# Layer 3's expert dispatch split by batch, the first half moved into the attention stream; two weight loads of layer 0 ordered behind a store

## The chip, the cores and the metric

The kernel runs on one core of one Trainium2 chip. A core has TensorE (PE, with its weight loads shown as PEld), VectorE (DVE), ScalarE (ACT), GpSimd (POOL) and SyncE (SP), each with its own in-order queue of instructions, and 16 DMA engines that all queues share. The metric is the device time of one launch in microseconds, lower is better.

## The reference

Four layers work on x, 2 batches of 512 tokens with 256 features (1024 tokens in all), in float32. Each layer adds a cross attention and then a mixture of experts, both on a layer norm of x:

```python
x = x + _L0_xattn_ref(_layernorm(x), ctx_1024, ...)
x = x + _L0_ffn_ref(_layernorm(x), ...)      # 8 experts, best one
x = x + _L1_xattn_ref(ctx_1024, _layernorm(x), ...)
x = x + _L1_ffn_ref(_layernorm(x), ...)      # best one, and a shared expert
x = x + _L2_xattn_ref(_layernorm(x), ctx_1024, ...)
x = x + _L2_ffn_ref(_layernorm(x), ...)      # two best of 8
x = x + _L3_xattn_ref(_layernorm(x), ctx_1024, ...)
x = x + _L3_ffn_ref(_layernorm(x), ...)      # two best of 8
```

The last one is what most of the change is about:

```python
h = rmsnorm(x @ W_in.T, in_norm_w)
logits = h @ Wr.T
_, idx = jax.lax.top_k(logits + expert_bias, TOP_K)     # TOP_K = 2
g_topk = jax.nn.softmax(jnp.take_along_axis(logits, idx, axis=-1), axis=-1)
...
for e in range(8):
    oe = rmsnorm(silu(h @ Wg[e].T) * (h @ Wu[e].T) @ Wd[e].T, enorm_w[e])
    out = out + gates[:, e:e + 1] * oe
s_hat = rmsnorm(out, out_norm_w) @ W_out.T
```

Layer 3's attention has 16 heads of 16 features over 1024 context rows, with rotary keys and queries.

## The kernel before

**Tokens and experts.** The 1024 tokens stand in X as 8 tiles of 128 rows, tiles 0 to 3 the first batch, 4 to 7 the second. An expert layer doesn't compute all experts for all tokens. It sorts: the *dispatch* gives each pick (token, expert) a slot, scatters the token's row to that slot of a DRAM tensor xd, and the experts then work on tiles of 128 slots. The first 8 tiles (`front`) belong to the 8 experts, one each; what an expert has beyond 128 rows goes to overflow tiles, whose weights are fetched by an indirect load on POOL with the expert's row in `wrow`. `ALWAYS` overflow tiles are worked on without a test (13 in layer 3), the rest only if `used` says so.

**The dispatch of layer 3 before.** It follows the attention and is done for all 8 tiles in one string: layer norm (`normed`), transposes (`to_T`), the product with W_in (`ph`), squares and root (`rms`, whose roots are `recip_sqrt`, line 62), the scaled rows `h`, transposes again, `router_logits` (`pl`), `two_best`, `two_gates`, and `slots_of`: a matmul with the triangle `below` and eight with `ones` (`pr`) count how many picks of each expert stand before a token, from which come overflow, fronts, slots, `wrow` and `used`. `moe` then issues 16 indirect DMAs on POOL (line 429), one for each pick and tile. Ahead of the second pick's eight, DVE writes another index into the last column of `h`, which must wait for the first pick's scatter of that tile to land. The first expert tile reads its slots back (`xs`, line 455) after all scatters.

**The attention of layers 2 and 3, `attend16`.** It works on 8 groups (batch, 4 heads), 16 slots each for layer 3. PE's order is written out by hand (`pe_in_order`): in each slot two score matmuls of the first pass (line 1394; DVE takes the maxima, line 1404), two of the second pass of an earlier group (line 1451; ACT takes the exponentials, line 1452), and a product with the values (line 1427). All PE results except the product rotate through seven PSUM banks of one tag (`bank`). Between slots stand *pieces*: short steps of generators in a queue (`Pieces`), such as the next group's queries (`prep`: pq, rot) and, after the first batch's last group, its four output projections (`add_out`: po). After the last first-pass slot (128) some 18 slots of second pass remain, then the last group's end and the second batch's projections.

**Layer 0's experts.** They use half tiles for two experts at a time (`pair_tile`, the first matmuls at line 489) in turn with overflow tiles (`slot_tile`). Before them, the filler `first_batch` computes keys and values of layer 1 for the first batch (`ahead1`): PE into a bank, ACT copies to `sk` or `sv` (two buffers), and ACT's queue issues the store to `kd` or `vd`. The weights `w` have four buffers. Two are loaded early; for the third and fourth, an overflow tile's (POOL) and one of the second pair's (SP), `behind_slots` makes them wait for the first read of slots, so that this one is not behind them:

```python
tc.add_manual_dep(
    x, first_slots[0].name, ...,
    reason="not among the transfers that the first tile waits for",
)
```

Where a scheduler may choose, it orders each engine's instructions when the kernel is built.

Of the kernel before, what the change touches and what calls it, by code (L numbers as in the profile page):

```python
# [33 lines left out]
def tile_kernel(ctx: ExitStack, tc: tile.TileContext, d: dict, out: bass.AP):  # L34
# [49 lines left out]

    def norm_to(dst, src, norm, ts=None, split=False):


        t0, mv, r = norm
        if split:
            nb = small.tile([P, mv.shape[1]], F32, tag=f"nb{mv.shape[1]}", name="nb")  # L90
            nc.vector.scalar_tensor_tensor(nb, mv[:, :, 0], -1.0, r, ALU.mult, ALU.mult)
        for t in range(mv.shape[1]) if ts is None else ts:
            if split and t % 2:
                nc.scalar.activation(
                    dst[:, t0 + t, :], src[:, t0 + t, :], AF.Identity, bias=nb[:, t : t + 1], scale=r[:, t : t + 1]
                )
                continue
            nc.vector.tensor_scalar(
                dst[:, t0 + t, :], src[:, t0 + t, :], mv[:, t, 0:1], r[:, t : t + 1], ALU.subtract, ALU.mult
            )  # L100
# [102 lines left out]
    class Pieces:  # L203
# [14 lines left out]
        def share(self, places):  # L218

            self.due += max(self.left, 0) / places  # L220
            while self.due >= 1.0:
                self.due -= 1.0
                self()
# [6 lines left out]
    def run_stream(n_groups, slots, lag, unit, prep, steps):  # L230


        pieces = Pieces()
        t = 0
        while t < n_groups * slots + lag or pieces.queue:
            n, u = divmod(t, slots)
            if u == 0 and n + 1 < n_groups:
                pieces.add(prep(n + 1), steps(n + 1))
            unit(t, pieces)
            if u == slots - 1:  # L240
                pieces.drain()
            t += 1


    def bc8(a):
        return a[:, :, None].to_broadcast([P, TT, E])

    def rt(name, shape=(TT, E)):
        return small.tile([P, *shape], F32, tag=f"rt_{name}", name=name, bufs=1)

# [34 lines left out]
    def two_gates(lg, oh1, oh2):  # L285

        t = rt("pick")
        s = rt("sel", (2, TT))
        for i, oh in enumerate((oh1, oh2)):
            nc.vector.tensor_mul(t, oh, lg)  # L290
            nc.vector.tensor_reduce(s[:, i, :], t, AX.X, ALU.add)
        m = rt("selm", (TT,))
        nc.vector.tensor_tensor(m, s[:, 0, :], s[:, 1, :], ALU.max)
        for i in range(2):
            nc.vector.tensor_sub(s[:, i, :], s[:, i, :], m)
        nc.scalar.activation(s, s, AF.Exp)
        nc.vector.tensor_add(m, s[:, 0, :], s[:, 1, :])
        nc.vector.reciprocal(m, m)
        for i in range(2):
            nc.vector.tensor_mul(s[:, i, :], s[:, i, :], m)  # L300
        return [s[:, i, :] for i in range(2)]


# [104 lines left out]

    def moe(L, ps, hp, ep, rows, slots, wrow, used, F, act, glu, finish, filler=None, hold=None, between=None):

# [8 lines left out]

        put, out_of = [], []  # L420
        named = len(slots) == 2
        RW = D + named
        for i, si in enumerate(slots):
            if named and i == 0:
                nc.vector.tensor_copy(rows[:, :, D], c_tok)
            for t in range(TT):
# [7 lines left out]
                put.append(x)  # L434
        if filler is not None:
            filler()
        wd = d[f"{L}_experts"]
# [4 lines left out]
        def behind_slots(x):  # L442

            tc.add_manual_dep(
                x, first_slots[0].name, mybir.DependencyInfo(mybir.DependencyClass.Sync, mybir.DependencyReason.DATA),
                reason="not among the transfers that the first tile waits for",
            )

# [205 lines left out]
    def ahead1(ps, st, w, cT, b, part=slice(None)):  # L654

        if b == 0:
            kds["L1"] = dram.tile([B * 4 * P, S], F32, tag="L1kd", name="kd")
            vds["L1"] = dram.tile([B * S, 512], F32, tag="L1vd", name="vd")

        def values(pv, kt):  # L660
            r = slice(b * S + kt * P, b * S + (kt + 1) * P)
            mm2(pv, cT, r, w, slice(512, 1024))
            v = st.tile([P, 512], F32, tag="sk", name="sv", bufs=2)
            nc.scalar.copy(v, pv)
            nc.scalar.dma_start(vds["L1"][r, :], v)

# [4 lines left out]
        jobs += [("v", kt) for kt in range(8)]  # L671
        ahead(ps, st, "L1", w, cT, jobs[part], values)

    def ahead16(ps, st, L, params, nkt):
# [58 lines left out]
    def fill_slots():  # L733
# [15 lines left out]
        for to in todo:  # L749
# [7 lines left out]
            )  # L757
            ins = yield

    def psum(tags, name):  # L760
# [271 lines left out]
    with (  # L1032
# [3 lines left out]
        psum(2, "L0fps") as ps,  # L1036
    ):
        rw = load_rows(fp, d["L0_ffn_router_w"], "rw")
        rb = load_bc(fp, d["L0_ffn_router_b"], "rb")
# [15 lines left out]
        def first_batch():  # L1055
            to_T(ps, cT, C, CT, g_c, b_c, "g")
            ahead1(ps, hp, wkv, cT, 0)

# [238 lines left out]

    def attend16(L, params, nkt, causal, rotary, bias, first=None, late=None):

# [10 lines left out]
        with (  # L1310
# [196 lines left out]
            with pe_in_order():  # L1507
                while t <= NG * slots + LAG + 6 or pieces.queue:
# [26 lines left out]
                    if k == 6 and 0 < m < NG:  # L1535
                        divide(m - 1)
                        if groups[m - 1][1] == 3:
                            pieces.add(add_out(groups[m - 1][0]), 4)

                    if h == 0 and 0 < n <= NG:  # L1540
# [11 lines left out]
    with (  # L1552
# [3 lines left out]
        psum(2, "L1fps") as ps,  # L1556
    ):
        rw = load_rows(fp, d["L1_ffn_router_wT"], "rw")
        xn = normed(fp, False)
# [27 lines left out]
    pre, params = params16("L3", True, False)  # L1587
    ap = pre.enter_context(tc.tile_pool(name="L3a", bufs=1, reuse_waits="tile"))
    first = {}
    with (  # L1590
# [3 lines left out]
        psum(2, "L2fps") as ps,  # L1594
    ):
        rw = load_rows(fp, d["L2_ffn_gate_wT"], "rw")
        xT = fp.tile([P, 2, NT], F32, tag="xT", name="xT")
# [11 lines left out]
        yd = moe("L2", ps, hp, ep, xn, slots, wrow, used, 1024, AF.Relu, False, plain, next_keys, hold)  # L1609
        add_results(results(ap, yd, 0, 4), gates, X, range(4))  # L1610
        late = results(ap, yd, 4, 4), gates


    attend16("L3", params, 8, False, True, False, first, late)
    pre.close()
    ctxr.close()
    with (
# [4 lines left out]
    ):  # L1622
        w_in = load_rows(fp, d["L3_ffn_W_inT"], "w_in")
        w_out = load_rows(fp, d["L3_ffn_W_outT"], "w_out")
        rw = load_rows(fp, d["L3_ffn_WrT"], "rw")
        eb = load_bc(fp, d["L3_ffn_expert_bias"], "eb")
        inw = load_bc(fp, d["L3_ffn_in_norm_w"], "inw")
        onw = load_bc(fp, d["L3_ffn_out_norm_w"], "onw")

        def mean_squares(ss, src):  # L1630

            sq = hp.tile([P, D], F32, tag="sq", name="sq")
            nc.scalar.activation(sq, src, AF.Square, accum_out=ss)  # L1633

        def rms(t, w, t0, n):

            ss = small.tile([P, n], F32, tag=f"ss{n}", name="ss")
            for i in range(n):
                mean_squares(ss[:, i : i + 1], t[:, t0 + i, 0:D])
            r = recip_sqrt(ss, n, 1.0 / D, RMS_EPS)  # L1640
            for i in range(n):
                nc.vector.scalar_tensor_tensor(
                    t[:, t0 + i, 0:D], t[:, t0 + i, 0:D], r[:, i : i + 1], w, ALU.mult, ALU.mult
                )

        xT = fp.tile([P, 2, NT], F32, tag="xT", name="xT")
        to_T(ps, xT, normed(fp, False), TT)
        h = fp.tile([P, TT, D + 1], F32, tag="h", name="h")
        for t in range(TT):
            ph = ps.tile([P, D], F32, tag="mm", name="ph")  # L1650
            mm2(ph, xT, slice(t * P, (t + 1) * P), w_in, slice(0, D))
            nc.scalar.copy(h[:, t, 0:D], ph)
        rms(h, inw, 0, TT)
        hnT = fp.tile([P, 2, NT], F32, tag="hnT", name="hnT")
        to_T(ps, hnT, h, TT)
        lg = router_logits(ps, hnT, rw)
        lb = rt("lb")
        nc.vector.tensor_add(lb, lg, eb[:, None, :].to_broadcast([P, TT, E]))
        oh1, oh2 = two_best(lb)
        gates = two_gates(lg, oh1, oh2)  # L1660
        slots, wrow, used = slots_of(ps, [oh1, oh2], 15)

        def normalise(yo, y, w):
            ss = small.tile([P, 1], F32, tag="ss1", name="ss1")
            mean_squares(ss, y)
            r = recip_sqrt(ss, 1, 1.0 / D, RMS_EPS)
            nc.vector.scalar_tensor_tensor(yo, y, r[:, 0:1], w[:, 6144:6400], ALU.mult, ALU.mult)

        yd = moe("L3", ps, hp, ep, h, slots, wrow, used, 1024, AF.Silu, True, normalise)
        acc = fp.tile([P, TT, D], F32, tag="acc", name="acc")  # L1670
        outv = out.flatten_outer_dims().rearrange("(t p) f -> p t f", p=P)
        for t0 in range(0, TT, 2):
            add_results(results(hp, yd, t0, 2), gates, acc, range(2), True)
            rms(acc, onw, t0, 2)
            pt = ps.tile([P, 2, 2, P], F32, tag="mm", name="pt")
# [8 lines left out]
            nc.vector.tensor_add(X[:, t0 : t0 + 2, :], X[:, t0 : t0 + 2, :], po)  # L1684
            nc.sync.dma_start(outv[:, t0 : t0 + 2, :], X[:, t0 : t0 + 2, :])


# [170 lines left out]
```

## Time and profile before

| | us |
|---|---|
| median of 3 runs | 2259.86 (2259.75 to 2261.13) |
| the profiled execution | 2264.73 |
| its span, first to last instruction | 2262.7 |
| PE busy | 2070.5 (92%) |
| DVE busy | 1083.6 (48%) |
| ACT busy | 859.6 (38%) |
| POOL busy | 439.3 (19%) |
| layer 0's experts, first pair's first matmul | at 529.0 |
| layer 3's stream, eight groups | about 1634 to 1922 |
| layer 3's experts, first matmul | at 1994.7 |

The busy times are averages over stages with different limits, so they don't say which engine ends a stage. For that one looks at the stretch in question: the chain that ended last names at each moment what the end waited for, and the timeline shows each instruction with the idle time before it and what ended it. The mean granted clock of TensorE over the span is 0.95 of full speed; in stretches where it has little to do, it is about 0.5.

### The profile page before, as it was taken

To read this page: it belongs to the slowest core of one execution; us is meant where nothing else is said; L and a number is where in the kernel's file an instruction comes from. 1 tells how busy PE (TensorE), PEld (TensorE's weight loads), DVE (VectorE), ACT (ScalarE), POOL (GpSimd) and SP (SyncE) were. 2 spreads that over 40 slices of the span, in tenths; PEclk is the share of its full clock that TensorE was granted. 3 is DMA by queue.
4 is the path that set the end of the run, shared out by engine and by line. 5 is a ranking of instruction groups with operands and counts; after the bars stand their busy time and mean duration, and the time that the engine had idled before them with its cause. 6 is when DMAs were issued, how large, how long until landed. Compare 5 with 4: busy or idle time off the path is not lost. (4 is left out here: it accounts for less than half of the span.)

```text
span 2262.7 us, 29983 instructions
## 1 busy us (share of the span) xinstructions
PE 2070.5 (92%) x11532; PEld 1218.9 (54%) x11532; DVE 1083.6 (48%) x2157; ACT 859.6 (38%) x1645; POOL 439.3 (19%) x420
## 2 busy tenths in 40 slices
PE   7999999987998999999998998899699999579996
PEld 3444444353674444545586344599433333479995
DVE  7666666740125656655213884110377773322223
ACT  4444444421115565555112333222135556223333
POOL 2222223210012112111101122322123310111110
PEclk9999999988998999999899998999789999689998
DMA  4222222257945011001464512688310101547872
GB/s 129 71 62 75 71 75 58 87 208 298 372 146 121 29 34 39 21 11 65 142 231 146 202 35 79 221 310 312 104 47 30 34 15 25 248 180 297 321 303 64
DMA packets 111703, 300.72 MB, mean 133 GB/s; under 512 B 23232, under 2 KB 76224, under 8 KB 102848
## 3 DMA queue, kind: packets, MB, share of 16 engines
q1 hardware_dynamic: 76048, 159.30, 21.1%
q0 software_dynamic: 9888, 104.49, 11.9%
q10 hardware_dynamic: 25616, 34.90, 4.2%
q8 instruction: 97, 1.59, 0.3%
q14 instruction: 54, 0.44, 0.1%
HBM read 242.93 MB, written 47.66 MB: 128 GB/s over the span
## 5 line engine op out<-in xcount | busy, mean ns | idle before, releaser
L1452 ACT ACTIVATE p<-s 128x512 f32<-128x512 f32 (+3 forms) x384 | 185.9, 545 | 176.3 <-PE s L1451 114.8
L1394 PE MATMUL s<-kT,qT 32*128 32x512 f32 (+3 forms) x768 | 217.4, 612 | 8.7 <-DVE nm L1400 4.6
L132 PE MATMUL pa<-sT,w 128*128 128x128 f32 x1664 | 204.7, 278 | 8.0 <-DVE sT L466 3.7
L132 PEld LDWEIGHTS pa<-sT,w 128*128 128x128 f32 x1664 | 197.0, 193 | 16.4 <-ACT sq L1633 5.8
L561 PE MATMUL y<-w,hT 128*128 128x256 f32 x832 | 194.1, 386 | 7.2 <-ACT hT L551 3.3
L1451 PE MATMUL s<-qA,kT 32*128 32x512 f32 (+3 forms) x768 | 196.4, 587 | 1.2 <-ACT p L1452 0.9
L1404 DVE TENSOR_REDUCE mx<-s 128x1 f32<-128x512 f32 x256 | 163.6, 685 | 56.1 <-PE s L1394 35.5
L561 PEld LDWEIGHTS y<-w,hT 128*128 128x128 f32 x832 | 155.7, 193 | 30.0 <-DVE hT L558 5.2
L1139 ACT ACTIVATE p<-s,nm 128x512 f32<-128x512 f32 x192 | 129.5, 686 | 83.8 <-DVE nm L1136 83.8
L969 ACT ACTIVATE p<-s 128x1024 f32<-128x1024 f32 x128 | 124.1, 1021 | 89.9 <-PE s L964 89.9
L970 DVE TENSOR_SCALAR p<-p 128x1024 f32<-128x1024 f32 x128 | 107.3, 846 | 95.9 <-ACT p L969 95.7
L1136 DVE TENSOR_REDUCE nm<-s 128x2 f32<-128x1024 f32 x96 | 113.2, 1221 | 83.1 <-PE s L1132 83.1
L149 POOL TENSOR_TENSOR kT<-kT,turned 128x512 f32<-128x512 f32 x62 | 100.6, 1629 | 215.3 <-DVE turned L147 209.2
L975 DVE TENSOR_TENSOR acc<-acc,p 128x1024 f32<-128x1024 f32 x96 | 132.6, 1381 | 2.8
L895 PE MATMUL o<-p,v 128*64 128x512 f32 x512 | 125.9, 609 | 3.8 <-DVE p L970 3.8
L132 PE MATMUL pg<-sT,w 128*128 128x128 f32 x1056 | 129.0, 275 | 0.0
L964 PE MATMUL s<-qT,kT 64*128 64x512 f32 x512 | 127.2, 615 | 0.0
L558 DVE TENSOR_TENSOR hT<-act,pg 128x512 f32<-128x512 f32 x66 | 45.2, 688 | 167.9 <-PE pg L132 148.8
L132 PEld LDWEIGHTS pg<-sT,w 128*128 128x128 f32 x1056 | 123.6, 192 | 0.0
L148 POOL TENSOR_TENSOR kT<-kT,cos 128x512 f32<-128x512 f32 x62 | 87.9, 1427 | 134.7 <-DMA turned<-kT 61.2
L1427 PE MATMUL o<-p,v 128*32 128x256 f32 (+3 forms) x1280 | 106.6, 404 | 6.7 <-POOL p L1456 6.5
L1153 PEld LDWEIGHTS pt<-ident,p 128*128 128x128 f32 x768 | 85.9, 141 | 49.8 <-issue 24.7
(295 smaller groups left out, 3054.3 us busy)
## 6 DMA issues: line engine op xcount, KB each, us to landing
w<-in_L_experts_dram SPq DMA_DIRECT2D x8, 3200.0 KB
w<-in_L_experts_dram SPq DMA_DIRECT2D x8, 3072.0 KB
w<-in_L_experts_dram SPq DMA_DIRECT2D x8, 2048.0 KB
w<-in_L_experts_dram SPq DMA_DIRECT2D x8, 1536.0 KB
kd<-sk ACTq DMA_DIRECT2D x40, 256.0 KB
kT<-kd SPq DMA_DIRECT2D x16, 512.0 KB
turned<-kT SPq DMA_DIRECT2D x60, 128.0 KB
v<-vd SPq DMA_DIRECT2D x12, 512.0 KB
```

The source lines that it names most:

```text
L132: nc.tensor.matmul(ps_ap, lhsT[:, dc, lcols], rhs[:, dc, rcols], start=(dc == 0), stop=(dc == 1))
L561: nc.tensor.matmul(y, hT[:, f, :], w2[:, f, :], start=(f == 0), stop=(f == FT - 1))
L895: nc.tensor.matmul(G[n]["o"][64 * j : 64 * j + 64, :], V[g, b][:, kt, pr * P + 64 * j : pr * P + 64 * j + 64], p[:, j, :], start=(kt == 0) ...
L964: nc.tensor.matmul(s1[:, j, :], G[n]["kT"][r, kt * P : (kt + 1) * P], G[n]["qT"][r, :], start=True, stop=True)
L969: G[n]["exp"] = nc.scalar.activation(p, s1, AF.Exp, scale=0.125).ins
L975: nc.vector.tensor_add(G[n]["acc"], G[n]["acc"], p)
L1136: nc.vector.tensor_reduce(nm[:, qt, :, c], s1, AX.X, ALU.max, negate=True)
L1139: nc.scalar.activation(p[:, j, :], s1[:, j, :], AF.Exp, bias=nm[:, qt, j, c : c + 1], accum_out=l[:, qt, j, c : c + 1],)
L1394: nc.tensor.matmul(s1[:, :w], qT[r, qt * P : (qt + 1) * P], kT[r, c * 512 : c * 512 + w], start=True, stop=True)
L1404: nc.vector.tensor_reduce(mx[:, qt, j, c : c + 1], s1, AX.X, ALU.max)
L1451: nc.tensor.matmul(s2[:, qs], kT[r, kt * P : (kt + 1) * P], qA[r, qs], start=True, stop=True)
L1452: nc.scalar.activation(p[:, j, qs], s2[:, qs], AF.Exp, scale=0.25)
```

## The change

1. `behind_slots` adds a second dependency: the load also waits for the last of the stores that the filler issued (`stored[-1]`, the eighth value store of `ahead1`). In layer 0 this holds for the two loads named above.
2. Layer 3's dispatch becomes a class that works on one batch of four tiles. `dispatch3(0, ...)` is a generator that `attend16` puts into its pieces after the first batch's output projections, with one idle step (`gap`) after three of its stages. It is spread over the stream's last two groups of first-pass slots; its scatters are issued after them. `dispatch3(1, ...)` follows the attention, and works out how the second batch's rows fit behind the first's. `last` finds the overflow tiles' experts. Overflow tiles are handed out to the first batch first; their number stays the same.
3. What goes with it: W_in, the router's weights and two vectors are loaded before the stream, into a pool at the other end of the memory; the first batch's temporary tiles use the four buffers of the results loaded late (`yg`), which get a pool of their own; routing tiles come from the layer's pool and no longer from a permanent one.

In each engine's order, the first batch's steps now stand between attention slots on PE, about two slots apart. ACT loads its function table four times more, for two roots among the exponentials. On SP, layer 3's first key tiles go ahead of the rotated ones, and the fourth weight load of layer 3's experts stands behind the first three reads of slots. In layer 0 the slot read of the second pair stands ahead of its put-off load.

```diff
     def behind_slots(x):
-            tc.add_manual_dep(
-                x, first_slots[0].name, ...
-            )
+            for y in (first_slots[0], stored[-1]):
+                tc.add_manual_dep(
+                    x, y.name, ...
+                )
...
+    class Dispatch:
+        def wait(self, b):
+            for _ in range(self.gap if b == 0 else 0):
+                yield
+        def turned(self, dst, src, bank):
+            for dc in range(2):
+                pt = bank("pt")
+                for i in range(4):
+                    nc.tensor.transpose(pt[:, i * P : (i + 1) * P], src[:, i, dc * P : (dc + 1) * P], ident)
+                copy_alt(dc, dst[:, dc, :], pt)
+                yield
+        def norm(self, b, pool, bank, tags=("xn", "xT")):
+            S = self.S[b]
+            S["rows"] = pool.tile([P, 4, self.width], F32, tag=tags[0], name="xn")
+            norm_to(S["rows"][:, :, 0:D], X, norm_of(X, 4 * b, 4), d0=0)
+            yield
+            yield from self.wait(b)
+            S["xT"] = pool.tile([P, 2, 512], F32, tag=tags[1], name="xT")
+            yield from self.turned(S["xT"], S["rows"], bank)
+        def logits(self, b, srcT, w, bank):
+            pl = bank("pl")[:, 0 : 4 * E].rearrange("p (t e) -> p t e", e=E)
+            for t in range(4):
+                mm2(pl[:, t, :], srcT, slice(t * P, (t + 1) * P), w, slice(0, E))
+            self.S[b]["lg"] = rt_of_batch(b, "lg")
+            nc.vector.tensor_copy(self.S[b]["lg"], pl)
+            yield
+            yield from self.wait(b)
+        def to_slots(self, b, picks, bank):
...
+            nc.tensor.matmul(pr, below, oh[:, 4:9, :], start=True, stop=False)
+            for k in range(1, 5):
+                nc.tensor.matmul(pr, ones, oh[:, 4 - k : 9 - k, :], start=False, stop=(k == 4))
...
+            for i, si in enumerate(S["slots"]):
+                if named and i == 0:
+                    nc.vector.tensor_copy(rows[:, :, D], c_tok[:, 4 * b : 4 * b + 4])
+                for t in range(4):
+                    if i == 1:
+                        c = 4 * b + t
+                        nc.vector.tensor_scalar(rows[:, t, D:], c_tok[:, c : c + 1], float(NT), None, ALU.add)
+                    x = nc.gpsimd.indirect_dma_start(
+                        out=xds[self.L][0], out_offset=bass.IndirectOffsetOnAxis(ap=si[:, t : t + 1], axis=0),
+                        in_=rows[:, t, :], in_offset=None,
+                    ).ins
...
-            nc.scalar.dma_start(vds["L1"][r, :], v)
+            stored.append(nc.scalar.dma_start(vds["L1"][r, :], v).ins)
...
                         if groups[m - 1][1] == 3:
                             pieces.add(add_out(groups[m - 1][0]), 4)
+                            if dispatch is not None:
+                                pieces.add(dispatch(bank), 15)
...
+    far, dp = apart("L3d")
+    disp = Dispatch("L3", 2, 1)
+    w_in, rw = load_rows(dp, d["L3_ffn_W_inT"], "w_in"), load_rows(dp, d["L3_ffn_WrT"], "rw")
...
+    def dispatch3(b, pool, bank, tags, hpool):
+        S = disp.S[b]
+        yield from disp.norm(b, pool, bank, tags[:2])
+        h = S["rows"] = hpool.tile([P, 4, D + 1], F32, tag="h", name="h")
+        for k in range(2):
+            ph = bank("ph").rearrange("p (t f) -> p t f", t=2)
+            for i in range(2):
+                c = (2 * k + i) * P
+                mm2(ph[:, i, :], S["xT"], slice(c, c + P), w_in, slice(0, D))
+            nc.scalar.copy(h[:, 2 * k : 2 * k + 2, 0:D], ph)
+            yield
+        rms(pool, tags[2], h, inw, 0, 4)
+        yield
+        yield from disp.wait(b)
+        hT = pool.tile([P, 2, 512], F32, tag=tags[3], name="hT")
+        yield from disp.turned(hT, h, bank)
+        yield from disp.logits(b, hT, rw, bank)
+        lb = rt_of_batch(b, "lb")
+        nc.vector.tensor_add(lb, S["lg"], eb[:, None, :].to_broadcast([P, 4, E]))
+        picks = two_best_of_batch(b, lb)
+        S["gates"] = two_gates_of_batch(b, S["lg"], picks)
+        yield
+        yield from disp.to_slots(b, picks, bank)
+
+    attend16(
+        "L3", params, 8, False, True, False, first, late, lambda bank: dispatch3(0, ay, bank, ["yg"] * 4, dp)
+    )
...
+        all_of(dispatch3(1, fp, banks(ps), ["xn", "xT", "sq", "hT"], fp))
+        disp.last()
...
+        yd = moe(
+            "L3", ps, hp, ep, None, [], disp.wrow, disp.used, 1024, AF.Silu, True, normalise, sent=disp.put
+        )
```

## The prediction

> **What bounds the kernel now.** I read the page first: span 2262.7 us, TensorE (PE) busy 92% of it. Then the chain that ended last, for the order of the stages around the change, then the timeline of the two stages that it touches, and the busy time by stretches. All sums below are made against this one profiled execution. It took 2264.73 us (its span and 2.0 us around it), 4.9 us above the median of the runs, 2259.86; I take the difference that I work out off the median.
>
> First, layer 0's experts. The timeline, columns start, duration, engine, line and operation; in brackets the idle time before it and what ended it:
>
> ```profile
> 511.09 0.33 SPq L475 DMA_DIRECT2D w<-in_L_experts_dram  x1
> 511.09 0.36 ACTq L665 DMA_DIRECT2D vd<-sv  x1
> ...
> 511.98 0.98 POOL L536 DMA_INDIRECT w<-in_L_experts_dram,wrow  x1 [5.92 <-DMA vd<-sv]
> 512.36 0.33 ACTq L665 DMA_DIRECT2D vd<-sv  x1
> ...
> 528.40 0.59 ACT L664 COPY sv<-pk 128x512 f32<-128x512 f32 x1 [16.07 <-DMA vd<-sv]
> ...
> 529.03 3.68 PE L489 MATMUL pa<-w,sT 128*64 128x512 f32 x8 [12.13 <-ACT sv L664]
> ...
> 545.98 2.05 PE L132 MATMUL pa<-sT,w 128*128 128x128 f32 x16
> ```
>
> Two weight loads of 3.07 MB start at 511.1 and 512.0. The store of 256 KB issued at 511.09 lands only at 528.3, where the ones before it took 2.1 and 2.9 us. ACT's next copy needs its buffer, PE needs the bank that the copy frees, so PE stands still for 12.1 us.
>
> Second, layer 3. The chain that ended last (start, duration, step): the attention's groups begin at the pq rows; then the attention's end and the dispatch.
>
> ```profile
> 1730.10 1.91 PE pq L132 x4
> ...
> 1761.74 1.91 PE pq L132 x4
> ...
> 1793.39 1.91 PE pq L132 x4
> ...
> 1810.38 1.92 PE po L1487 x8
> 1815.79 1.92 PE po L1487 x8
> 1821.21 1.92 PE po L1487 x8
> 1826.62 1.92 PE po L1487 x8
> 1832.52 1.91 PE pq L132 x4
> ...
> 1950.86 7.01 PE pl L132 x32
> ...
> 1969.70 1.01 POOL xd L429
> ...
> 1988.77 2.51 DMA xd<-h,si
> 1991.40 1.98 DMA xs<-xd
> 1994.71 3.77 PE pa L132 x16
> ```
>
> A group takes 31.6 us, and 39.1 us where four projections of 1.92 us stand in it: 7.5 us more for 7.7 us of PE work. PE is the bound there. From the last sum of the attention (1930.72) to the first expert matmul (1994.69), 64 us, PE waits for a string of small steps.
>
> ```profile
> 1850.00:1860.00 10.00, 10.00 (x99) 3.03 (x91) 7.32 (x13) 5.94 (x12) 1.28 (x1) 1.00 0.01 2
> 1950.00:2000.00 50.00, 17.97 (x85) 16.70 (x84) 12.03 (x76) 4.45 (x6) 15.45 (x16) 0.51 0.41 161
> ```
>
> Columns: length, then busy us of PE, weight load, DVE, ACT, POOL, then granted clock, DMA share, GB/s. In the stream DVE has 27% and ACT 41% to spare; in the dispatch PE works 18 of 50 us at clock 0.51.
>
> **Part 1, layer 0: the loads wait for the last store.** The two loads (one on SP, one on POOL) move behind the eighth store. Undisturbed, copies and stores alternate at what the first four show: store 3 lands about 2.3 us after its issue, copy 5 at 513.4, copy 8 at 517.7 (its matmul ends at 516.6), store 8 issued 518.3, landed about 520.6. PE then starts the pair at about 517.4, 11.6 us earlier. The pair takes 13 us (the next two pairs: 13.6 and 12.8; this one took 17.0 at a lower clock and with waits), so PE wants the next tile at 530.5. That tile's weights are what was put off: both loads leave at 520.6, and the same two with the stores took 17 us before (511 to 528.5, 412 to 446 GB/s). They land at about 537. So the stall doesn't vanish: it is 6.5 us in front of the tile that began at 545.98, and the gain is 9 us. Behind the waiting load on SP stand the slot reads of later tiles (one read, that of the second pair, is moved ahead of it) and the second pair's other load. That one needs a buffer that is free at 530.5, shares the queues with its fellow, and lands near 551; the second pair, 561.06 before, finds it then. The 9 us stay. On POOL only later loads queue. Bounds: 0 (loads landing at 546) to 12.
>
> **Part 2, layer 3's tail: half the dispatch.** By steps, before -> after: last sum to first transpose 1.9 -> 2.3 (other rows stand between on DVE); transposes and copies 3.8 -> 3.2; W_in and squares, paced by ACT at 0.86 per tile, 8.6 -> 5.8; root and scaling 1.35 the same; transposes and copies 4.5 -> 3.1; logits 7.0 -> 3.5; two best 3.9 -> 3.7 (as many instructions, half as wide, 0.22 each); ranks, 18 -> 10 matmul records, 4.1 -> 2.4; slots 3.8 -> 5.4, since the second batch's string has 33 DVE rows to the first index in place of 22, at 0.16; scatters, 16 -> 8 at 1.27, from the first to the last issue 19.1 -> 8.9; last scatter to first expert matmul 5.9 the same. Sum 64.0 -> 45.6: gain 18.4 us. Bounds 16 to 20. One of four weight loads of layer 3 now stands behind three slot reads on SP. It is needed for tile 3, 33 us after the start, and such a load takes 11 us in the median, 21 at most: nothing, unless the reads themselves are late.
>
> **Part 3, layer 3's stream: the first batch is added.** PE: 16 transposes (nmT x4 takes 0.6) 2.4; W_in, 16 records as po, 3.8; logits, 16 records (32 take 4.17 in layer 2) 2.1; ranks, 10 records (18 take 2.1 there) 1.2. Sum 9.5 us at full clock, all on the bound. Eight scatters (10 us of POOL) and the index rows fall after the last first-pass slot. POOL has only one division behind them, needed at the stream's end some 18 us later; DVE, waiting for the scatters to land before it writes the second index, has a reciprocal behind it. If that cover fails, up to 7 us. DVE gets about 13 us of new work (the two blocks of small operations are 3.7 and 3.5), ACT 10.5, four table loads of 1.28 among them. Both fit the spare time of two groups on average (63 us: 17 and 26), but not locally: seven banks are turned over in under two slots (2 us each), and products need the exponentials of the slot before.
>
> [...] The trace, in layer 3's experts:
>
> ```profile
> 2008.06 1.28 ACT L62 ACT_TABLE_LOAD   x1
> ...
> 2009.35 0.20 ACT L62 ACTIVATE rsq<-rsq 128x1 f32<-128x1 f32 x1
> 2009.58 1.28 ACT L557 ACT_TABLE_LOAD   x1
> ...
> 2010.87 0.60 ACT L557 ACTIVATE act<-pa 128x512 f32<-128x512 f32 x1
> ```
>
> A root between exponentials holds ACT from 2008.06 to 2010.87, 2.8 us. [...] About 1 us of each blip is slack in a slot. [...] Stream: +13 us.
>
> [...]
>
> **Small edits.** The routing tiles change pools, which moves three memsets, and in layer 2 the scatter ahead of a POOL product; PE there has key projections until 1450, 11 us after the last scatter. Layer 3's stream loads key tiles ahead of the rotated ones, some 4 us later for those, needed about 30 us later. Four small loads of 0.4 MB go ahead of them. Cost 0, bounds -2 to +2.
>
> **Sum.** -9 - 18.4 + 13 = -14.4 us: 2245.5.
>
> **Rivals.**
> (a) The stall in layer 0 only changes its name: the put-off loads land at 546 or later, since three queues share the engines. For it: the loads were done 17 us before use, and now come just in time. Against it: two loads at 425 GB/s need 15 us and have 25. Gain 0 there: 2254.5.
> (b) Slower: the stream's seven banks. While DVE works through small operations or ACT reloads tables, no bank comes free, PE stands, and the time is not recovered because PE is the bound. If none of the new DVE and ACT work is hidden, the stream pays 9.5 + 13 + 10.5 = 33 us, the sum is +5.6: 2265.5. It decides once stalls pass 17.9 us. For it: in-order queues, and a DVE 73% busy. Against it: both fit on average, and PE's inserted steps stand two slots apart, so each input is done before its turn.
> (c) The stream absorbs more than the groups say (5 us in place of 13): -22.4, 2237.5.
> [...]
>
> **Chances.** Main 0.70 (own range 2239 to 2252), (a) 0.10, (b) 0.08, (c) 0.08, (d) 0.04. 0.2%, 4.5 us, is about what a measurement of this kernel can tell from no change. Faster: 0.70 + most of (a) + (c) = 0.87; same 0.05; slower 0.08. The range reaches to (c) and just past (a): 2237 to 2256.
>
> **What would show it.** Layer 0: idle before the first pa of the pair under 1 us, and about 6 us before the next tile's pa, ended by its weights. Stream: the two groups after the projections together 10 to 16 us longer than 63. Tail: 44 to 48 us from the last sum to the first expert matmul, with eight scatters. It is wrong if the expert tile of layer 0 starts no earlier than before, relative to the attention, or if those two groups take over 80 us.

## The result and the profile after

| | before | changed |
|---|---|---|
| median of 7 runs, us | 2259.75 (2257.26 to 2261.33) | 2272.15 (2267.51 to 2276.64) |
| the profiled execution, us | 2264.73 | 2273.33 |
| its span, us | 2262.7 | 2271.6 |

The ratio is 1.0055, 95% interval 1.0042 to 1.0068: 12.4 us slower, where 14.4 us faster was forecast. The same kernel was then run on four more chips, beside the kernel before each time, and there it was 6 to 10 us faster. So the question is what happened in the first comparison.

Layer 0 first, in the timeline of the changed kernel (start, duration, engine, line and operation; in brackets the idle time before it and what ended it):

```profile
510.96 0.33 ACTq L884 DMA_DIRECT2D vd<-sv  x1
...
512.48 1.94 PE L706 MATMUL pa<-w,sT 128*64 128x512 f32 x8 [0.56 <-issue]
...
513.67 0.33 ACTq L884 DMA_DIRECT2D vd<-sv  x1
...
515.71 0.33 SPq L692 DMA_DIRECT2D w<-in_L_experts_dram  x1
...
516.64 0.98 POOL L753 DMA_INDIRECT w<-in_L_experts_dram,wrow  x1 [15.55 <-DMA vd<-sv]
...
534.06 3.75 PE L133 MATMUL pa<-sT,w 128*128 128x128 f32 x16 [8.34 <-DMA w<-in_L_experts_dram,wrow]
```

The 12.1 us before the pair are gone (0.56), the last store leaves at 513.7, the loads follow it, and the stall is now 8.3 us before the tile. That is the mechanism foreseen.

Now layer 3, in the chain that ended last (start, duration, step), from the first batch's projections to the first expert matmul:

```profile
1815.59 1.93 PE po L1720 x8
1822.10 1.98 PE pq L133 x4
1847.49 1.92 PE ph L133 x8
1852.84 1.94 PE ph L133 x8
1875.99 1.90 PE pl L133 x16
1904.35 5.39 another core or an unknown queue
1911.93 2.01 PE s L1684 x4
...
1942.13 2.01 PE s L1684 x4
...
1950.05 8.25 PE po L1720 x32
...
1973.29 3.60 PE pl L133 x16
...
1996.17 2.48 DMA xd<-h,si
1998.77 2.13 DMA xs<-xd
2002.23 3.77 PE pa L133 x16
```

The dispatch's steps stand where they were expected, and the tail is short. What is new is a piece of 5.39 us that the profile can't name, and behind it score matmuls that follow each other every 3.0 us. In the timeline of that spot:

```profile
1903.25 1.10 ACT L1685 ACTIVATE p<-s 128x512 f32<-128x512 f32 x2
1903.75 1.13 PE L1684 MATMUL s<-qA,kT 32*128 32x512 f32 x4
...
1905.38 1.13 PE L1684 MATMUL s<-qA,kT 32*128 32x512 f32 x4
...
1907.00 0.96 POOL L480 DMA_INDIRECT xd<-h,si  x1 [0.31 <-issue]
...
1909.72 2.06 ACT L1685 ACTIVATE p<-s 128x512 f32<-128x512 f32 x4 [5.37 <-remote]
...
1910.37 1.56 PE L1660 MATMUL o<-p,v 128*32 128x256 f32 x8 [3.87 <-ACT p L1685]
1911.86 2.08 PE L1684 MATMUL s<-qA,kT 32*128 32x512 f32 x4
...
1914.88 2.08 PE L1684 MATMUL s<-qA,kT 32*128 32x512 f32 x4
```

ACT waits for PE's scores of 1903.75. They should be done by 1904.9. But the trace's record of PE's semaphore has a step at 1903.73 and the next one only at 1909.70, four within 0.2 us, and ACT starts 0.02 us behind that, at 1909.72. PE then waits for ACT. POOL, DVE and the DMA queues go on meanwhile. I call this *the hold*. Behind it each matmul takes twice as long: 2.08 us for four scores, 1.13 before.

The stretches (length, busy us of PE, weight load, DVE, ACT, POOL, granted clock, DMA share, GB/s), first of this execution, then of a later one of the same kernel on another chip (after_again below), which has no hold:

```profile
1900.00:1910.00 10.00, 6.48 (x48) 1.67 (x40) 0.87 (x5) 4.03 (x8) 6.13 (x7) 0.91 0.30 96
1910.00:1920.00 10.00, 9.63 (x40) 2.38 (x44) 0.00 (x0) 3.96 (x8) 1.27 (x1) 0.50 0.28 66
1920.00:1930.00 10.00, 10.00 (x46) 2.25 (x46) 0.00 (x0) 4.13 (x8) 0.00 (x0) 0.50 0.00 0
1930.00:1940.00 10.00, 10.00 (x42) 2.60 (x40) 0.00 (x0) 3.48 (x7) 0.00 (x0) 0.50 0.01 2
```

```profile
1900.00:1910.00 10.00, 9.98 (x74) 2.89 (x76) 0.87 (x5) 7.14 (x15) 5.78 (x6) 1.00 0.30 96
1910.00:1920.00 10.00, 10.00 (x74) 2.75 (x74) 0.00 (x0) 6.75 (x13) 1.26 (x1) 1.00 0.27 67
```

From 1920 to 1940 PE is busy 10 of 10 us, as it is without the hold from 1910 to 1920, but at half clock, with 42 to 46 records where the other has 74. In the stretch of the hold itself, 1900 to 1910, both moved 96 GB/s. From the query projection of the sixth group (pq) to the sum of the last group (sm), the stream takes 159.5 us before, 175.1 without the hold, and 197.3 here.

### The profile page after: what moved, and what is told of

Read it like the earlier page. It is cut to its first block, busy times and chain, and to the rows that moved or that the text cites. A ratio compares the mean times of both kernels' runs of the same rounds, so it can differ in the third digit from the quotient of the medians.

```text
span 2271.6 us, 30058 instructions
## 1 busy us (share of the span) xinstructions
PE 2084.6 (92%) x11534; PEld 1217.7 (54%) x11534; DVE 1095.2 (48%) x2226; ACT 862.3 (38%) x1644; POOL 439.2 (19%) x420
## 5 line engine op out<-in xcount | busy, mean ns | idle before, releaser
L1627 PE MATMUL s<-kT,qT 32*128 32x512 f32 (+3 forms) x768 | 223.4, 624 | 10.0 <-DVE nm L1633 4.5
L1684 PE MATMUL s<-qA,kT 32*128 32x512 f32 (+3 forms) x768 | 210.4, 623 | 1.5 <-DVE qA L1648 1.5
L1660 PE MATMUL o<-p,v 128*32 128x256 f32 (+3 forms) x1280 | 114.7, 431 | 10.5 <-POOL p L1689 6.6
L1627 PEld LDWEIGHTS s<-kT,qT 32*128 32x128 f32 x768 | 78.3, 193 | 68.1 <-issue 28.3
```

The source lines that it names most:

```text
L1627: nc.tensor.matmul(s1[:, :w], qT[r, qt * P : (qt + 1) * P], kT[r, c * 512 : c * 512 + w], start=True, stop=True)
L1660: nc.tensor.matmul(G[n]["o"][32 * j : 32 * j + 32, qs], G[n]["v"][:, kt, g % 2 * 4 + j, :], p[:, j, qs], start=(kt == 0 and half != 1), st ...
L1684: nc.tensor.matmul(s2[:, qs], kT[r, kt * P : (kt + 1) * P], qA[r, qs], start=True, stop=True)
```

## The experiments

Theory A: a hold of PE at the stream's end brings PE's clock down; the second pass alone doesn't bring it back; hold and half clock cost about 22 us. Without them the change does what was worked out. Rivals: the change itself is slower, through its steps on PE, DVE and ACT or through its scatters; or any hold costs as much, wherever it stands.

Times below are medians, and ratios are to the kernel before on the same chip, with 95% intervals.

**1. Each half alone: l0_only, l3_only, l0_only_2.** l0_only is the kernel before with the two dependencies of `behind_slots`; l3_only is the changed kernel with this edit:

```diff
-            for y in (first_slots[0], stored[-1]):
+            for y in (first_slots[0],):
```

> Before with layer 0's edit alone (two weight loads wait for the last store). Theory A, the traces of before and after: the first pair begins 16.6 us earlier and the tile after it 11.9 us earlier, and that stays to the end: 12 us faster than before, 2248. Rival: what stood at -12 behind layer 0 in the one trace was partly the clock of the stages around it: 0 to 6 us faster, 2254 to 2260.

> The changed kernel without layer 0's edit. Theory A (the stream of layer 3 lost 37 us in the traces, the tail gave back 19): 22 to 25 us slower than before, 2283, with PE at half clock for some 40 us at the end of layer 3's stream again. Rival (the half clock of that stretch was an accident of one execution): about 5 us slower than before, 2265, and 1.62 us for each slot of the second pass at the end.

> Before with layer 0's edit alone, once more, beside the changed kernel. Theory (layer 0 gives 7 us in the traces, layer 3 about 5): 4 to 7 us faster than before, and 0 to 5 us slower than the changed kernel where that has no hold. Rival (layer 3's part gives nothing): as fast as the changed kernel without the hold.

Layer 0 alone: 2253.35, ratio 0.9980 (0.9966 to 0.9994), and on another chip 2251.65, 0.9972 (0.9960 to 0.9984). Layer 3 alone: 2254.68, 0.9988 (0.9974 to 1.0002). So layer 0 gives 4.5 to 6.3 us in time. Layer 3's part is not 22 us slower, and its trace has neither hold nor half clock at the stream's end: its stream takes 175.1 us. That was the first sign that the program alone doesn't bring the hold.

**2. The changed kernel again: late_scatter, after_again, after_3, after_4.** late_scatter was to send the first batch's scatters only after the attention. But the order is chosen by the scheduler, which put them back: each engine has the same instructions in the same order as in the changed kernel. It is read here as another run of that kernel.

> The changed kernel with the first batch's eight scatters sent only after the attention, ahead of the second batch's dispatch; nothing is left out. Theory A (the scatters' traffic held PE from 1905.9 to 1910.4 and so brought the clock down for the last 37 us): the stream is 20 us shorter, the tail about 10 us longer, 2262. Rival B (the hold and the clock come from the dispatch's other steps, its blocks of small DVE operations and its roots): stream as in the changed kernel, tail 10 us longer, 2282.

> The changed kernel as it is, beside the other three on one chip. Theory A (in the first comparison of the two, 2272 against 2260, each execution of the changed kernel lost about 20 us to a hold of PE at the end of layer 3's stream and to the half clock behind it, and this goes with the chip or the hour, not with the program): where the profile shows no hold there, it is 6 to 12 us faster than before; where it shows one, 12 us slower. Rival (the program itself is slower): 12 us slower with or without a hold.

> The changed kernel once more, on whichever chip comes. Theory A (the hold at the end of layer 3's stream goes with the chip or the hour): either about 2250, 6 to 9 us faster than before, with slots of 1.62 us at the stream's end, or about 2272 with slots of 3.0 us behind a hold; nothing between. Rival (the first comparison was slow for another reason): a time or a profile that fits neither.

> The changed kernel on whichever chip comes. Theory A (the hold goes with the chip or the hour): about 2250 with slots of 1.62 us at the end of layer 3's stream, or about 2272 with a hold and slots of 3.0 us. Rival: a time between, or one of the two without its profile.

| run | time | ratio | sixth pq to sm |
|---|---|---|---|
| late_scatter | 2248.87 | 0.9957 (0.9944 to 0.9970) | 175.1 |
| after_again | 2251.55 | 0.9967 (0.9955 to 0.9979) | 175.2 |
| after_3 | 2250.16 | 0.9971 (0.9957 to 0.9986) | 175.0 |
| after_4 | 2249.75 | 0.9967 (0.9954 to 0.9980) | 175.1 |

Four chips, 57 executions from 2241.5 to 2258.0, no hold in any of the four traces. In the first comparison all 7 executions lay at 2267.5 and above. The rival "the program itself is slower" is out for chips that don't show the hold.

**3. A hold made on purpose: forced_hold, hold_mid.** One product of PE gets one more wait. In forced_hold it is the fourth slot of the last group's second pass, which waits for the eighth scatter:

```diff
+                        if dispatch is not None and (m, k) == (NG - 1, 3):
+                            tc.add_manual_dep(held[0], disp.put[7].name, ...)
```

> The changed kernel with one wait added: the attention product of the fourth slot of the last group waits for the eighth scatter of the first batch. This makes a hold of PE of about 5 us where the trace of the changed kernel had one. Theory A (such a hold brings the clock down, and the second pass alone does not bring it back): the slots behind it take 3.0 us in place of 1.62, and the time is 5 + about 17 = 20 us or more above the changed kernel's on the same chip. Rival (the clock comes back within 7 us, as elsewhere in the trace): 5 to 8 us above it.

2275.4, ratio 1.0074 (1.0052 to 1.0095), 23.9 us above after_again on the same chip. The timeline:

```profile
1905.53 1.13 PE L1686 MATMUL s<-qA,kT 32*128 32x512 f32 x4
1911.75 1.08 PE L1661 MATMUL o<-p,v 128*32 128x256 f32 x8 [5.10 <-DMA xd<-h,si]
1912.76 2.08 PE L1686 MATMUL s<-qA,kT 32*128 32x512 f32 x4
...
1915.78 2.08 PE L1686 MATMUL s<-qA,kT 32*128 32x512 f32 x4
```

5.1 us of waiting, then slots of 3.02 us to the end. The stream takes 197.4 us; the first comparison's took 197.3. In hold_mid the fifth slot of the fourth group's second pass waits for the third group's divisors, where both passes run:

```diff
+                        if dispatch is not None and (m, k) == (3, 4):
+                            for y in spreads[-4:]:
+                                tc.add_manual_dep(held[0], y.name, ...)
```

> The changed kernel with a hold of PE made on purpose in the middle of layer 3's stream, where both passes run: the product of the fifth slot of the fourth group's second pass waits for the four transfers that spread the third group's divisors, some 5 us. Theory A (both passes together bring the clock back, the second pass alone does not): the hold, and 3 to 7 us at half clock behind it: 6 to 10 us above the changed kernel's 2249 to 2252. Rival (any hold of that length costs the 24 us that the one at the end cost): 2273 to 2276.

```profile
1768.34 1.08 PE L1663 MATMUL o<-p,v 128*32 128x256 f32 x8 [8.22 <-DMA rec<-inv]
...
1771.37 1.08 PE L1663 MATMUL o<-p,v 128*32 128x256 f32 x8
...
1774.10 0.64 PE L1663 MATMUL o<-p,v 128*32 128x256 f32 x8
...
1775.90 0.64 PE L1663 MATMUL o<-p,v 128*32 128x256 f32 x8
```

This hold came out longer, 8.2 us, but the product takes 1.08 us only twice and 0.64 from the third slot on: the clock is back after some 6 us (0.68 from 1760 to 1770, 0.81 from 1770 to 1780, 1.00 behind that). 2260.92, ratio 1.0015 (1.0000 to 1.0031), some 11 us above the changed kernel's ratio elsewhere, a little more than expected and far from the rival's 24. Its stream takes 186.9 us, 11.8 above 175.1: the hold and 3.6 us. So the longer hold costs less than half of the shorter. It is the place that makes it dear: behind the hold where only the second pass runs, the half clock stayed (0.50 from 1910 to 1950 in forced_hold). That it is the mix of matmuls at the place, and nothing else there, is argued from these two places.

**4. Dense matmuls behind the hold: burst, burst_again, burst_4.** All three are the changed kernel with this:

```diff
+                    if dispatch is not None and m == NG - 1 and 2 <= k < 6:
+                        warm = bank("warm")
+                        for dc in range(2):
+                            nc.tensor.matmul(warm, ident, xT[:, dc, 0:512], start=(dc == 0), stop=(dc == 1))
```

> The changed kernel with eight added 128-row matmuls of 512 columns (two in each of four slots) in the last group's second pass; their result is not used. Theory A (the clock had fallen and stays down because the 32-row matmuls of the second pass alone do not bring it back; dense matmuls do): 3.5 to 7 us of added work, then slots of 1.62 in place of 3.02 us for the 12 that remain, 17 us back: about 10 us faster than the changed kernel, 2262. Rival B (the low clock has another cause and stays): 4 to 7 us slower than the changed kernel, 2277 to 2279.

> The changed kernel with eight dense matmuls in four slots of the last group, as before. Theory A: where the changed kernel beside it has the hold and the half clock, it is about 10 us faster than that; where it has none, 4 to 7 us slower, the price of the matmuls (in the run before it stood 6 us above the same program without them).

> The changed kernel with eight dense matmuls in four slots of the last group's second pass, beside the changed kernel. Theory A: about 10 us faster than that where it has the hold, 4 to 7 us slower where it has none.

2255.0, 2258.02 and 2257.29, ratios 0.9995, 1.0001 and 1.0001: 6.1, 6.5 and 7.5 us above the changed kernel beside each. None of these chips showed the hold, so whether dense matmuls would have ended the half clock was not tested. What they do show is the price of PE work in this stream: 4 x 2.0 us of added matmuls cost nearly all of their 8 us.

**5. Where the dispatch stands: end_scatter, l3_end, gap0.** end_scatter really puts the eight scatters behind the attention, by a dependency on its last sum:

```diff
+                    if b == 0:
+                        tc.add_manual_dep(x, ends[-1].name, ...)
```

> The changed kernel with the first batch's eight scatters and their rows of DVE behind the attention's last sum. Theory A (the scatters' traffic is what holds PE): no hold at the stream's end, in any execution, and a tail longer by what of the eight scatters (10 us) isn't hidden behind the second batch's norm, W_in and logits, 0 to 4 us. Rival (the hold does not come from the scatters): time as the changed kernel's plus 0 to 4 us, hold included where that has one.

2263.8, ratio 1.0022 (1.0010 to 1.0033), 12.3 us above after_again on that chip. Both expectations fell: I had hidden the scatters behind the second batch's work, but the index rows of DVE between them wait for landings, and stand ahead of that work on DVE. The tail grows from 43.4 to 58.8 us, and the stream keeps its 175.2: sent this late, the scatters take away what the dispatch in the stream gives. As this chip doesn't show the hold, the run says nothing of what the scatters have to do with it.

l3_end takes the first batch's dispatch out of the stream:

```diff
-        ... first, late, lambda bank: dispatch3(0, ay, bank, ["yg"] * 4, dp)
+        ... first, late
...
+        all_of(dispatch3(0, fp, banks(ps), ["xn0", "xT0", "sq0", "hT0"], dp))
         all_of(dispatch3(1, fp, banks(ps), ["xn", "xT", "sq", "hT"], fp))
```

> The changed kernel with the first batch's dispatch taken out of layer 3's stream and done per batch after the attention, ahead of the second's. Theory (the working of the prediction as the clean traces have it: the stream pays about 15 us for the first batch, the tail gets back about 20): the stream is 15 us shorter, the tail 20 us and more longer, so 5 to 12 us above the changed kernel. Rival (the in-stream part costs more than it gives): at or below the changed kernel's 2249 to 2252.

2258.5, ratio 0.9998 (0.9987 to 1.0009). The stream is back at 159.6 us, the tail is 67.4. Against the changed kernel's ratios on other chips it is 6 to 9 us slower, as the theory had it. gap0 sets the pause to nothing (`Dispatch("L3", 2, 0)`):

> The changed kernel with no pause between the dispatch's steps in the stream (a gap of 0 pieces in place of 1), so that its steps come about two slots earlier each. Theory: PE's 9.9 us of steps stay; less time stands between a step and the one that needs it, so PE waits up to 3 us more for DVE and ACT, and the scatters begin some 8 us earlier, partly where both passes still run: 0 to 3 us above the changed kernel on chips without the hold. Rival (the pause is only lost distance): same as the changed kernel.

2255.84, ratio 0.9992 (0.9985 to 1.0000), about 6 us above the changed kernel's ratio: more than expected. Its stretches:

```profile
1870.00:1880.00 10.00, 9.74 (x50) 2.54 (x42) 7.21 (x24) 3.37 (x8) 1.26 (x1) 0.70 0.08 27
1880.00:1890.00 10.00, 9.66 (x58) 3.85 (x58) 5.51 (x22) 3.06 (x6) 3.89 (x4) 0.61 0.12 41
```

The steps crowd, the clock is lower (0.70 and 0.61 over 20 us), and the stream takes 183.4 us in place of 175.1. The pause is worth its slots.

**6. The kernel before, again: before_again.**

> The kernel before, looked at a second time. Its first profiled execution took 2264.7, 5 to 7 us above its medians on three chips. Theory: that execution was a long one (228.6 us of its span at half clock, where the versions profiled since had 173 to 202), so some 4 us of what stands against it around layer 0 and again around layer 2's dispatch is not the change's: a second one should show the 12 us stall of layer 0 again and a total of 2257 to 2260. Rival: stretches and total as in the first, 2263 to 2266.

One execution of 2260.2, span 2258.3: 4.4 us shorter than the first trace. It is 7.5 us ahead at the first value store of layer 0 and has lost 3.4 of that by the end of layer 2. Layer 0's stall is there again (the pair's tile 38.6 us after the first value store, 38.2 in the first trace), and so are 159.5 us of stream and 64.1 of tail. Layer 3's stages repeat to 0.2 us, layer 0's from the first store on to 1.3 us; the total of the first trace was long ahead of them.

**7. Layer 0's stall before the tile: tile_first, tile_first_early.** In tile_first the second pair's load waits for the tile's weights too; in tile_first_early the tile's load doesn't wait for the store:

```diff
                 if s > 0:
-                    behind_slots(x)
+                    behind_slots(x, stored[-1], put_off[0])
...
-                    behind_slots(x)
+                    behind_slots(x, stored[-1])      # tile_first_early: behind_slots(x)
+                    put_off.append(x)
```

> The changed kernel with the second pair's weight load (on SP) waiting for the tile's weight load as well, so that the tile's 3.07 MB come alone behind the last store. In the traces of the changed kernel the two loads start at 515.7 and 516.6 and land together at 534, and PE stands for 8.3 us before the tile. Theory (the two loads share the engines, so one alone takes about half): the tile's weights land at 524 to 526, the stall before it goes, the second pair's loads land at 541 to 543 and are wanted at about 542: 6 to 8 us faster than the changed kernel, about 0.993 of before on a chip without the hold. Rival (the second pair's load, now late, becomes the stall): no faster than the changed kernel, 0.997.

> As the version beside it, but the tile's load no longer waits for the last store (it starts at 512, beside the stores), and only the second pair's load waits. Theory (a store is held up by each load beside it): one load beside the stores holds the pair up by about half of the 11.5 us that two did, some 6 us, while the tile and second pair come earlier: 0 to 5 us slower than the version beside it. Rival (one load beside the stores does them no harm): as fast or faster than the version beside it.

2272.82, ratio 1.0080 (1.0059 to 1.0100), and 2270.1, 1.0075 (1.0051 to 1.0098). The reason isn't layer 0. On this chip, the sixth of the experiments, the hold is back, in both traces. tile_first at its spot:

```profile
1914.79 2.06 ACT L1688 ACTIVATE p<-s 128x512 f32<-128x512 f32 x4 [5.37 <-remote]
...
1915.44 1.56 PE L1663 MATMUL o<-p,v 128*32 128x256 f32 x8 [3.85 <-ACT p L1688]
```

The same 5.37 us as in the first comparison; PE's semaphore stops 5.7 us after the first scatter's issue there and here; then slots of 3.0 us follow; both streams take 195.7 us, and all 12 executions lie between 2265.5 and 2278.3. Times can't judge the two versions of layer 0 then, only traces. With tile_first the tile starts 24.9 us after the first store in place of 30.8, but the second pair then waits for its own load, and the layer's last product comes 154.3 us after the first store in place of 149.5: the rival. With tile_first_early it is 149.2, no different from the changed kernel and ahead of tile_first: the rival again. The stall moves; that the two loads of 3.07 MB cost that much in any order is a reading, not shown.

## Why the prediction was wrong

By its own steps, in us against before. "Without the hold" is the five traces l3_only, late_scatter, after_again, after_3 and after_4 (layer 0 without l3_only); where they differ, their mean.

| step | forecast | without the hold | first comparison |
|---|---|---|---|
| layer 0, first store to last expert product | -9 | -7 | -6.3 |
| layer 3's start, last product of layer 2 to the sixth pq | 0 | +3.8 | +4.3 |
| stream, sixth pq to sm | +13 | +15.6 | +37.8 |
| tail, last sum to first expert matmul | -18.4 | -21 | -20.5 |
| layer 3's experts | 0 | +1 | +1.8 |
| sum | -14.4 | -8 | +17 |
| measured, by the ratio | | -6.5 to -9.7 (four chips) | +12.4 |

The last column is one profiled execution against another and the table leaves out the other stages, which together were 8 us shorter than in the long trace of before: the two spans differ by 8.9 us, the medians by 12.4.

**The step that failed** is the stream's, and in it the stalls. I costed each PE step "at full clock", added small stalls, and took it that a stall costs its own length. Here it didn't: the clock of the matmuls behind it fell too, from 1.00 before 1908.2 to 0.50 from 1910 to 1950. The +13 us have 3.5 us for stalls beside the 9.5 us of PE steps, and no run shows that figure: without the hold the stalls cost 5.7 us, and in the first comparison the stream's 37.8 us less 9.9 us of PE steps make 27.9 us of them, eight times as much. Behind a hold of 4 to 6 us, the slots left of the second pass went from 1.62 to 3.02 us: 1.4 us each, some 17 us, with the hold 22. forced_hold shows that size (197.4 us of stream) and hold_mid that it depends on the place. The hold itself was not among the waits that the prediction thought of, and its cause is open. Rival (b) came near in time for another reason: it had banks blocked by DVE and ACT, but without the hold all stalls together cost 5.7 us (15.6 less the 9.9 us of PE steps), far from the 17.9 at which it was to decide.

It could have been seen. Part 1 of the prediction counts a lower clock behind layer 0's stall (with waits, 17.0 us for a pair that otherwise takes 13); part 3 puts it at nothing. And in the trace of before, layer 3's stream begins with first pass alone, where PE runs its scores from 1642.3 to 1657.3 without a break:

```profile
1640.00:1650.00 10.00, 10.00 (x39) 5.26 (x40) 8.38 (x15) 0.59 (x1) 7.30 (x6) 0.84 0.00 0
1650.00:1660.00 10.00, 10.00 (x32) 5.11 (x28) 9.54 (x18) 0.59 (x1) 0.20 (x1) 0.50 0.65 211
```

The same of the changed kernel (after_again):

```profile
1640.00:1650.00 10.00, 10.00 (x32) 5.78 (x30) 10.00 (x18) 0.59 (x1) 0.00 (x0) 0.50 0.68 220
```

PE is busy 10.00 of 10.00 us in all three, and the clock goes down to 0.50 and stays there: in this attention a busy PE is no proof of a fast one, and the first pass alone didn't raise the clock there. (DVE, at 9.54 and 10.00, may set the pace there, so this stretch doesn't show what the half clock costs.) The prediction took the clock from the stretch in use (1.00 at 1850) and didn't ask what a stall at 1905, with the first pass over, would do to it.

**Point by point.**

- *Layer 0*: mechanism right, size a little off. PE starts the pair as forecast and takes 13 us for it; the loads take 18 us, not 16.5, and the stall before the tile is 8.3, not 6.5. Rival (a) fell.
- *Tail*: right, and a little better. 43.4 us where 45.6 was forecast (44 to 48), eight scatters in 8.9 us.
- *Roots*: the row was right. ACT is held 2.8 us by a root, as the row said, and PE waits 0.7 us beside the first and 1.2 beside the second, for DVE each time (after_again). The working has a slip: 2.8 us less the 1 us of slack, an estimate, is 1.8, so the two roots alone make 3.6 us, all of the 3.5 that the +13 us have for stalls, and nothing is left there for DVE's blocks.
- *Matmul busy time*: the groups were right (7.5 us more for 7.7 us of PE work before). 9.9 us of inserted steps cost 15.6, and the 8 us of burst cost 6 to 7.5. Rival (c) fell.
- *Small edits at 0*: missed. Layer 3's start costs 3.3 to 4.3 us in the traces of the table, 3.1 in l3_end's, and between 1.7 and 4.1 in the others with its new order. PE waits 1.0 us for maxima behind DVE's work on rotated keys, and half clock lasts 24 to 27 us there in place of 17 (after_again and before_again). How much of it each reordered load or row makes wasn't tried.
- *Range*: without the hold the medians, 2248.9 to 2251.6, lie inside 2237 to 2256; the time of the first comparison doesn't.

**What stays open.** What holds PE's semaphore was not found. It came in the one trace of the first comparison and in both on the sixth chip of the experiments, each time at the same spot of the scatters; it came in none on the five chips between, though five of those traces have the scatters in that spot and nothing added to the stream (l3_only, late_scatter, after_again, after_3 and after_4), and four of the five are of the very program that had it first. The kernel before, run beside those that had the hold, took its usual time each time (2259.75 in the first comparison, 2254.7 on the sixth chip). So it takes the changed stream as well as a certain chip or hour. Which part of the changed stream is open: that the scatters cause it is a guess, since no version with the dispatch in the stream and its scatters elsewhere met such a chip.

## What to carry to other kernels

Here a stall in a stretch that PE bounds cost its length and, as it brought the clock down, more time behind it: 17 us behind a stall of 5.1 in one place, 3.6 behind one of 8.2 in another. How much went with when the clock came back: at 1950.2, some 38 us behind the stall, in the first place, after some 6 us in the second. So read the granted clock of every stretch of the same kind before costing a new wait, above all where the stream thins out. Where both passes run, a wait was the cheaper one here, so risky steps (scatters, waits on other queues) are better tried there. When a result stands against the working by less than 1%, run the same program on more chips before explaining it: here the same instructions were 6 to 10 us faster on four chips and 12 us slower in the first comparison. Layer 0's edit alone, 4.5 to 6.3 us faster on two chips, leaves the stream as it was before, and the kernel before was not slowed where the hold came.

## What the hardware showed that was not expected

- **A busy PE that stays at half clock.** Behind the hold PE was busy 10.00 of 10.00 us at clock 0.50 from 1920 to 1940 in the first comparison, and from 1920 to 1950 in forced_hold. In the first comparison the clock is 1.00 until 1908.2 and 0.50 from 1908.3 on, 1.7 us after the scores of 1905.38 should have ended; in forced_hold it is 0.96 from 1900 to 1910 and 0.50 behind that, in hold_mid 0.68 from 1760 to 1770. In hold_mid it came back after some 6 us, but not with the second pass alone, with its matmuls of 32 rows or 32 columns: there the clock came back only when the scores were over, at 1950.2 in forced_hold, within the last 24 products, and at 1952.6 in the first comparison, within the projections (`po`). The same second pass, entered at full clock, kept it to the stream's end (after_again: 1.00 from 1900 to 1930).
- **Dips without an idle gap.** In every trace with the dispatch in the stream the clock falls soon after the logits, for 3.4 or 6.8 us and in gap0 for 13.7, though PE's longest wait there is 0.3 us: 0.83 in the stretch 1885 to 1895 of after_again. The fall at the start of before's stream, shown above, has no idle gap either. What brings these falls was not tested.
- **A late signal.** PE's semaphore stood still for 6.0 us (1903.73 to 1909.70) in the first comparison and again for 6.0 us in both traces of the sixth chip, while DVE, POOL and the DMA queues went on.
